# A recurrence, attention and routed experts on one core: warm-up products, chunk 0's sums on VectorE, a re-priced planner, earlier turns of small groups

## The chip, the core and the metric

One core of a Trainium2 chip. The time is that of one execution on the device in microseconds (us); several are made and their median is given. The engines are PE (TensorE), DVE (VectorE), ACT (ScalarE), POOL (GpSimd) and SP (SyncE, which here only issues DMAs). Each runs its own list of instructions in the order in which it was written, and waits for others by semaphores.

## What is computed

The input x has 4 sequences of 1024 tokens with 256 channels. Both halves have the same frame: normalise, compute, normalise, add.

```python
# first half: a recurrence over time, then gates
px = layernorm(x) @ W_state.T + b_state
g  = sigmoid(layernorm(x) @ W_gate.T + b_gate)
state = tanh(px[t] + state)              # 1024 steps, one after the other
x = x + layernorm(g * states)
# second half: causal attention (16 heads of 16 channels), then 4 experts
h = rms(layernorm(x), n1_w); q, k = rms(h @ wq.T), rms(h @ wk.T); v = h @ wv.T
y = layernorm(x) + softmax(causal(q @ k.T / 4)) @ v @ wo.T
w = top2(softmax(rms(y, n2_w) @ gate_w.T))   # two of four experts for each token
y = y + sum(w[e] * expert[e](rms(y, n2_w)))  # the first 64 channels get no addition
x = x + layernorm(y)
```

The experts have two to four layers.

## The kernel before

**Tiling.** Time is cut into 8 chunks of 128 steps. For each chunk: `projections` normalises x (bn_stats L449, scaling L521), turns it (L463, copied to SBUF by ACT and DVE in L472), multiplies it with `wsg` (L534, four banks of 128x512) and evicts states and gates (L552, L548 on DVE). `recurrence` makes the 128 steps: an addition of 128x8 on POOL (L583), then a tanh on ACT (L586; the very first is L579). `gates` makes two wide tanh per chunk (L567). `before` multiplies states by gates (L615), turns them (L623), normalises, adds x, normalises again and turns (L463). `heads` makes q, k and v (L711, L778; turns in L798). Attention runs over 32 tiles (chunk i, sequence b): scores in two layouts (L883), the maximum of one (L968, L975 on DVE), the exponential of the other (L1024 on ACT), sums with v (L1065), and `after` (L1084 to L1128) for the output. `experts_input` routes the chunk's tokens. A tile of chunk i has i + 1 key blocks, so chunk 7 is eight times chunk 0.

**Order.** No loop stands in the program: `Plan.run` writes it out. Every stage is a generator that yields an `Op` (engine, cost in us, priority, events that it reads, buffers that it needs); the planner keeps a clock for each engine and always takes the `Op` that can start first by its clocks, then the one of lower priority. Thus the costs decide only the order in each engine's list; on the chip each engine waits for real events. PE has seven banks of PSUM to hand out (`Banks`). Where the planner sees PE wait for more than 0.8 us between 60 and 420 us on its clock, `fill` puts products into the list that nobody uses (L417).

**Experts.** Tokens are sorted by their pair of experts: six kinds. For each kind, `groups` makes a body for its first 256 tokens, and further groups, each under a branch (L1728), as far as the number of tokens asks for them. A body fetches rows for later groups by indirect DMA from POOL (L1516), turns the next group's rows (`turn`: scaling on DVE L1531, transposes on PE L1538, copy on ACT L1544), and runs the layers (L1561, activations L1622, L1629 to L1638; last layer L1581, added by DVE in L1649). `last` normalises (L1662 to L1678, in between z and r on POOL, L1669 and L1670) and stores the rows by indirect DMA (L1681). A remainder of at most 128 tokens of a kind is its small group, the tail: `rwtail` holds its rows, `xtail` the turned ones. The six tails come after all bodies, each under a branch of its own (L1742):

```python
    for n, c in enumerate(order):
        hint(f"tail{n}", KINDS + c, 0)
        with tc.If(n_of[KINDS + c] > 0, preferred_fallthrough_block=True, label=f"tail{n}"):
            group(c, TAIL, [turn(c, TAIL)])
```

A tail thus fetches nothing (its rows come from the body after its kind's, the last kind's from its own), but it turns its rows itself before its first layer.

Of the kernel before, what the change touches and what calls it, by code (L numbers as in the profile page):

```python
# [18 lines left out]
P = 128  # L19
# [23 lines left out]
def kernel(  # L43
# [43 lines left out]
    nc.vector.tensor_scalar_mul(hb_g, vec[:, 6:8], 0.5)  # L87
# [10 lines left out]
    for arena, group in (  # L98
# [19 lines left out]
        tc, ident, mhalf, hb_g, route, keys, values,  # L118
# [18 lines left out]
LEAST = 0.8  # L137

# [33 lines left out]
class Op:  # L172
    def __init__(self, eng, cost, prio, reads=(), slots=(), banks=0, lag=0.0, either=(), ahead=0.0):
        self.eng, self.cost, self.prio, self.reads = eng, cost, prio, reads
        self.slots, self.banks, self.lag, self.either = slots, banks, lag, either
        self.ahead = ahead


class Plan:
# [13 lines left out]

    def ev(self, *key):
        return self.events.setdefault(key, Ready())

    def start(self, op):
# [7 lines left out]
        for b in self.banks.pick(op.banks):  # L205
            t = max(t, self.banks.free[b])
        return t
# [12 lines left out]
    def run(self, streams):  # L220
# [5 lines left out]
        while waiting:  # L226
# [19 lines left out]
            self.end = t + op.cost + op.lag  # L246
            try:
# [6 lines left out]
def sandwich(  # L254
    ctx, tc, ident, mhalf, hb_g, route, keys, values,
# [76 lines left out]
    def once():  # L332
# [4 lines left out]
        done("loaded")  # L337
        yield Op("DVE", 2.0, 50.0, [ev("st", 0)])
        nc.vector.tensor_copy(ident_h, ident)
# [20 lines left out]
        for p in pads.tiles:  # L360
            yield Op("DVE", 1.2, 50.0)


            nc.vector.memset(p, 0.0)
            nc.vector.memset(p[:, 1, :, HD : HD + 1], 1.0)
# [11 lines left out]
        for e in range(1, E):  # L377
# [3 lines left out]
        nc.gpsimd.memset(mask, 0.0)  # L381
        nc.gpsimd.affine_select(
            out=mask, in_=mask, pattern=[[-1, P]],
            compare_op=ALU.is_ge, fill=NEG, base=0, channel_multiplier=1,
        )
        nc.gpsimd.memset(late[:, : 3 * P], 0.0)

# [16 lines left out]
        )  # L404
        done("once")

    def fill(until):

        now = plan.clock["PE"]
        if not FILLED[0] <= now <= FILLED[1] or until - now < LEAST:  # L410
            return
# [16 lines left out]
    def newton(z, tag):  # L428

        n = z.shape[1]  # L430
# [4 lines left out]
        )  # L435
        nc.vector.tensor_scalar(z, z, -0.5, None, ALU.mult)
        for _ in range(3):
            nc.vector.tensor_tensor(t, y, y, ALU.mult)
            nc.vector.tensor_tensor(t, t, z, ALU.mult)
            nc.vector.scalar_tensor_tensor(y, t, 1.5, y, ALU.add, ALU.mult)  # L440
        return y

    def moments(prio, tiles, tag, reads):

        mv = stat.tile([P, len(tiles), 2], F32, tag=tag, name=tag)
        for n, t in enumerate(tiles):
            yield Op("DVE", 0.6, prio, reads)
            st6 = stat.tile([P, 6], F32, tag="st6", name="st6")
            nc.vector.bn_stats(st6, t)  # L449
            nc.vector.bn_aggr(mv[:, n, :], st6)  # L450
        return mv

    def transposed(prio, srcs, reads, name, ahead=0.0):
# [14 lines left out]
        for cc, (eng, copy) in enumerate(  # L468
            (("ACT", nc.scalar.copy), ("DVE", nc.vector.tensor_copy))
        ):  # L470
            yield Op(eng, 0.65, prio, [ev(name, "in PSUM")])
            copy(to[:, cc, : n * P], banks.tiles[bs[cc]][:, : n * P])  # L472
# [8 lines left out]
    def states(i):  # L481

        both = keys.rearrange("p b (h t) -> p (b h) t", h=NHC)[:, :, i * P : (i + 1) * P]
        return both[:, : NCC * B, :], both[:, NCC * B :, :]

# [10 lines left out]
    def projections():  # L496


        for i in range(NI):
            prio = 4.0 * i - 8.0  # L500
            while i not in xc_of:
                yield Op("DVE", 0.0, prio, [ev("x", i)])
            x_c = xcs.tiles[xc_of[i][1]]
            x_rows = [x_c[:, b, :] for b in range(B)]
            mv = yield from moments(
                prio, x_rows, "mv0", [ev("x", i), *([ev("av", B - 1)] if i >= AT_ONCE else [])]
# [3 lines left out]
            if i:  # L510
                yield Op("DVE", 2.2, prio)
                nc.vector.tensor_scalar(z, mv[:, :, 1], LN_EPS, None, ALU.add)
                r = newton(z, "r0")
# [5 lines left out]
            for b in range(B):  # L519
                yield Op("DVE", 0.35, prio, [ev("r0", i)])  # L520
                nc.vector.tensor_scalar(  # L521
                    x_rows[b], x_rows[b], mv[:, b, 0:1], r[:, b : b + 1],
                    ALU.subtract, ALU.mult,
                )
            done("ln", i)
            to, lnT_ = yield from transposed(prio, x_rows, [ev("ln", i)], f"lnT{i}")
# [3 lines left out]
            for half, dc in ((0, 0), (0, 1), (1, 0), (1, 1)):  # L530
# [15 lines left out]
                yield Op("DVE", 0.68, prio, [ev("pp", i, half, dc)])  # L546
                if half:
                    nc.vector.tensor_scalar(  # L548
                        tile, pb, 0.5, hb_g[:, dc : dc + 1], ALU.mult, ALU.add
                    )  # L550
                else:
                    nc.vector.tensor_scalar(tile, pb, b_s[:, dc : dc + 1], None, ALU.add)  # L552
                give(pp)
                if (half, dc) == (0, 1):
                    done("st", i)
# [14 lines left out]
    def recurrence():  # L570

        prev = None
        for i in range(NI):
            st, _ = states(i)
            last = ev("st", i)
            for t in range(P):
                if prev is None:
                    yield Op("ACT", 0.21, -9.0, [last])
                    nc.scalar.activation(st[:, :, t], st[:, :, t], AF.Tanh)  # L579
                else:  # L580
                    yield Op("POOL", 0.21, -9.0, [last])
                    s = sp.tile([P, NCC * B], F32, tag="s", name="s")
                    nc.gpsimd.tensor_tensor(s, st[:, :, t], prev, ALU.add)  # L583
                    done("s")
                    yield Op("ACT", 0.21, -9.0, [ev("s")])
# [8 lines left out]
            done("rec", i)  # L594

# [4 lines left out]
    def before():  # L600


        for i in range(NI):
# [36 lines left out]
            for b in range(B):  # L640
                row, = yield Op("DVE", 0.8, prio, [ev("r1", i), ev("x1in", i)], [rows])
# [52 lines left out]
    def heads(i, bs):  # L694
# [9 lines left out]
        for k, b in enumerate(bs):  # L704
# [12 lines left out]
            yield Op("ACT", 0.69, prio, [ev("pqk", i, b)])  # L717
# [4 lines left out]
            sq_, = yield Op("ACT", 0.62, prio, (), [sqs])  # L722
# [11 lines left out]
        for k, b in enumerate(bs):  # L734
            if len(bs) > 1:
                yield Op("DVE", 0.8, prio + b)
# [11 lines left out]
                "ACT", 0.69, prio + b,  # L748
                [ev("pk", i, b), *([ev("last read", i)] if i < NI - 1 else [])],
# [11 lines left out]
            yield Op("ACT", 0.69, prio + b, [ev("pq", i, b)])  # L761
# [10 lines left out]
    def value_rows(i, b):  # L772
# [13 lines left out]
        yield Op("DVE", 0.46, prio, [ev("pv", i, b)])  # L786
# [1016 lines left out]
```

## Time and profile before

| | |
|---|---|
| median of 3 runs | 1471.9 us (1470.63 to 1476.9) |
| the profiled execution | 1470.96 us; its span 1469.2 us |
| PE busy | 1311.5 us, 89% |
| DVE, ACT, POOL busy | 896.5, 705.7, 465.5 us |
| mean granted clock of PE | 0.947 |
| last step of chunk 0, 1, 7 | 88.1, 170.5, 741 us |

The span is that of the instructions; the rest of the time lies around it. Products are pipelined and their ends are modelled, so a busy PE is not PE at its peak, and the unused products of L417 count as busy (38.55 us). "<-" in the last brackets of a timeline row names what ended the idle time before it.

### The profile page before, as it was taken

What the parts mean: (1) busy time and instruction counts of PE and PEld (TensorE: products, weight loads), DVE (VectorE), ACT (ScalarE), POOL (GpSimd) and SP (SyncE); (2) the same over time, 40 slices, a digit from 0 to 9 for tenths busy, and PEclk for the clock granted to TensorE, in tenths of its full rate; (3) what the DMA queues carried; (4) which work ended last, traced back from release to release, by engine and by line L of the source; (5) the groups of instructions that cost most, each with busy time, mean ns of one, the idle gap of its engine ahead of it and who ended that gap; (6) DMA issues with size and microseconds to landing.
All of it is one profiled execution on the core that took longest, in us unless ns stands there. A gap on an engine that the chain in (4) does not pass through costs nothing. (4 is left out here: it accounts for less than half of the span.)

```text
span 1469.2 us, 43267 instructions
## 1 busy us (share of the span) xinstructions
PE 1311.5 (89%) x17455; PEld 1020.3 (69%) x17470; DVE 896.5 (61%) x2738; ACT 705.7 (48%) x2144; POOL 465.5 (32%) x1466
## 2 busy tenths in 40 slices
PE   4578797988999998999999999999899999999964
PEld 2235455666676676687677677878688889888764
DVE  5567568599688778778877987784614312113311
ACT  2345545655765765776665455657222222223211
POOL 2433534535444444334311101101233321214321
PEclk8799989999998989998999999999999999999987
DMA  3010010001010000001000100131122120103210
GB/s 128 23 50 2 4 42 17 16 3 46 3 31 17 3 22 28 3 3 46 3 4 5 45 3 4 38 105 62 55 84 64 54 66 26 40 23 83 55 43 5
DMA packets 35917, 49.57 MB, mean 34 GB/s; under 512 B 7638, under 2 KB 27862, under 8 KB 35670
## 3 DMA queue, kind: packets, MB, share of 16 engines
q1 hardware_dynamic: 28774, 25.20, 5.6%
q0 software_dynamic: 6624, 20.62, 5.0%
q8 instruction: 147, 2.41, 0.7%
q14 instruction: 100, 0.82, 0.2%
q10 hardware_dynamic: 272, 0.52, 0.1%
HBM read 32.87 MB, written 13.46 MB: 32 GB/s over the span
## 5 line engine op out<-in xcount | busy, mean ns | idle before, releaser
L1024 ACT ACTIVATE ex<-bank 128x512 f32<-128x512 f32 (+1 forms) x592 | 325.9, 582 | 153.4 <-PE bank L883 87.5
L883 PE MATMUL bank<-keys,q 32*128 32x128 f32 x4608 | 351.9, 293 | 17.4 <-ACT q L762 4.1
L583 POOL TENSOR_TENSOR s<-keys 128x8 f32<-128x8 f32 x1023 | 223.4, 218 | 384.8 <-ACT keys L586 374.1
L883 PE MATMUL bank<-q,keys 32*128 32x128 f32 x4608 | 333.9, 292 | 5.4 <-ACT ex L1024 2.8
L883 PEld LDWEIGHTS bank<-q,keys 32*128 32x128 f32 x4608 | 272.6, 191 | 75.7 <-issue 41.9
L586 ACT ACTIVATE keys<-s 128x8 f32<-128x8 f32 x1023 | 218.5, 214 | 212.1 <-POOL s L583 209.5
L883 PEld LDWEIGHTS bank<-keys,q 32*128 32x128 f32 x4608 | 292.2, 193 | 37.0 <-DVE nm L975 6.3
L975 DVE TENSOR_REDUCE nm<-bank 128x1 f32<-128x512 f32 (+4 forms) x336 | 203.0, 639 | 53.7 <-PE bank L883 44.5
L968 DVE CUSTOM_DVE_ANT_0 bank<-bank,late 128x512 f32<-128x512 f32 (+2 forms) x320 | 188.3, 622 | 48.7 <-PE bank L883 47.4
L1044 POOL TENSOR_SCALAR_AFFINE_SELECT ex<-ex 128x256 f32<-128x256 f32 (+1 forms) x240 | 102.7, 429 | 262.4 <-ACT ex L1024 261.4
L1065 PE MATMUL av<-ex,values 128*17 128x128 f32 x4608 | 175.0, 282 | 3.1 <-issue 1.2
L1561 PE MATMUL bank<-values,keys 128*128 128x256 f32 x568 | 133.5, 381 | 5.9 <-PEq L1728 3.0
L1065 PEld LDWEIGHTS av<-ex,values 128*17 128x17 f32 x4608 | 110.0, 99 | 40.3 <-issue 16.4
L1622 ACT ACTIVATE keys<-bank 128x256 f32<-128x256 f32 (+1 forms) x136 | 50.4, 371 | 149.8 <-PE bank L1561 149.7
L1561 PEld LDWEIGHTS bank<-values,keys 128*128 128x128 f32 x568 | 105.8, 190 | 21.7 <-issue 3.5
L1561 PE MATMUL bank<-keys 128*128 128x256 f32 x384 | 84.8, 379 | 0.0
L1561 PEld LDWEIGHTS bank<-keys 128*128 128x128 f32 x384 | 73.0, 190 | 9.9
L534 PE MATMUL bank<-big,wsg 128*128 128x512 f32 x128 | 64.0, 646 | 5.9 <-ACT big L472 5.9
L711 PE MATMUL bank<-wqk,big 128*128 128x512 f32 x128 | 65.7, 642 | 3.2 <-ACT big L472 3.2
L1649 DVE SCALAR_TENSOR_TENSOR rwnext<-av,rwnext 128x192 f32<-128x192 f32 x24 | 8.9, 414 | 93.4 <-PE av L1581 93.4
L1622 ACT ACTIVATE hid<-bank 128x256 f32<-128x256 f32 x66 | 25.3, 383 | 84.5 <-PE bank L1561 84.5
L1669 POOL TENSOR_SCALAR z<-mv 128x2 f32<-128x2 f32 (+1 forms) x18 | 4.1, 227 | 187.7 <-DVE mv L1663 178.4
(265 smaller groups left out, 1788.2 us busy)
## 6 DMA issues: line engine op xcount, KB each, us to landing
row_d<-xn SPq DMA_DIRECT2D x16, 512.0 KB
xn<-in_x SPq DMA_DIRECT2D x8, 512.0 KB
xc<-in_x SPq DMA_DIRECT2D x7, 512.0 KB
keys<-in_e_l SPq DMA_DIRECT2D x2, 1024.0 KB
keys<-in_e_w SPq DMA_DIRECT2D x2, 512.0 KB
keys<-in_e_down SPq DMA_DIRECT2D x2, 384.0 KB
wsg<-in_w_sg ACTq DMA_DIRECT2D x1, 512.0 KB
xc<-in_x SPq DMA_DIRECT2D x4, 128.0 KB
```

Of the source, the lines that this page charges most:

```text
L534: nc.tensor.matmul(pb, lhsT=wsg[:, cc, half * C + dc * P : half * C + (dc + 1) * P], rhs=lnT[:, cc, :], start=(cc == 0), stop=(cc == NCC - 1),
L583: nc.gpsimd.tensor_tensor(s, st[:, :, t], prev, ALU.add)
L586: nc.scalar.activation(st[:, :, t], s, AF.Tanh)
L711: nc.tensor.matmul(pqk, lhsT=hT[:, cc, b * P : (b + 1) * P], rhs=wqk[:, cc, :], start=(cc == 0), stop=(cc == NCC - 1),)
L883: nc.tensor.matmul(banks.tiles[pbs[j]][:, m * P : (m + 1) * P], lhsT=k if kind == "sT" else q, rhs=q if kind == "sT" else k, start=(m == 0 ...
L968: nc.vector.tensor_tensor_reduce(out=s_, in0=s_, in1=late[:, 4 * P - w :], scale=-1.0, scalar=FMAX, op0=ALU.add, op1=ALU.min, accum_out=by ...
L975: nc.vector.tensor_reduce(by_slot[:, half, h0:h1, 2 * p + j], banks.tiles[pb][:, m0 * P : m1 * P].rearrange("p (h w) -> p h w", h=h1 - h0) ...
L1024: nc.scalar.activation(exs.tiles[ex[1]][:, j, : step.w], banks.tiles[pb][:, : step.w], AF.Exp)
L1044: nc.gpsimd.affine_select(out=d, in_=d, pattern=pattern, compare_op=ALU.is_ge, fill=0.0, base=0, channel_multiplier=-1,)
L1065: nc.tensor.matmul(av[32 * j : 32 * j + HD + 1, hc, :], lhsT=v_all[:, b, kb, 4 * hc + j, :], rhs=exs.tiles[ex[j // 2][1]][:, j % 2, m * P ...
L1561: nc.tensor.matmul(hb[0].tiles[hb[1]][:, :w_], lhsT=w[:, j, m * P : (m + 1) * P], rhs=src[:, j, :w_], start=(j == 0), stop=(j == nk - 1),)
L1622: nc.scalar.activation(to, src, AF.Gelu)
```

## The change

Four parts; the new line of an old one is given where the prediction speaks of it.

1. *Start.* A new stream `begin` casts the identity to bf16 first and lets PE make 100 products of 128x128 with it that nobody uses. `hb_g` (half the gates' bias) is made after chunk 0's statistics instead of at the head of DVE's list. The states of chunk 0 are evicted in two pieces, the first 32 steps first, and the recurrence may begin after the first piece of the second bank. The mask is made first on POOL, and the memsets of the four `pad` tiles go from DVE to POOL. Fillers need the mask.
2. *Chunk 0's steps.* The addition of chunk 0 is made by DVE, of the other chunks by POOL. The projections of chunks 1 to 4, which fall beside it, are cut into small pieces on DVE.
3. *Planner.* Costs are split into the time that an engine is taken and a `lag` until the result is there, and most become smaller. A step announces when the next one is due (`every`: 0.45 us on DVE, 0.52 on POOL); another `Op` of that engine that would run into it waits until after the step, unless it is longer than the whole gap and starts right behind the last step.
4. *Tails.* Their rows are fetched and turned in the bodies of later kinds; the tail's own body turns nothing.

```diff
+SOONEST = 32
+BEFORE_ALL = 100
+BY_VECTOR = 1
+FITS = 0.05
+RIGHT_BEHIND = 0.06
...
+        if op.eng in self.chain and not op.every and op.cost:
+            ended, due, cost = self.chain[op.eng]
+            if t < due < t + op.cost - FITS and not (
+                op.cost > due - ended and t <= ended + RIGHT_BEHIND
+            ):
+                t = due + cost
         return t
...
             self.clock[op.eng] = t + op.cost
             self.end = t + op.cost + op.lag
+            if op.every:
+                self.chain[op.eng] = t + op.cost, t + op.every, op.cost
...
+    def begin():
+        yield Op("DVE", 0.2, -20.0)
+        nc.vector.tensor_copy(ident_h, ident)
+        done("ident")
+        pb, = yield Op("PE", 6.5, -20.0, [ev("ident")], banks=1)
+        for _ in range(BEFORE_ALL):
+            nc.tensor.matmul(
+                banks.tiles[pb][:, :P], lhsT=ident_h, rhs=ident_h, start=True, stop=True
+            )
+        give(pb)
+        yield Op("DVE", 0.2, -7.5, [ev("r0", 0)])
+        nc.vector.tensor_scalar_mul(hb_g, vec[:, 6:8], 0.5)
+        done("hb")
...
-        for p in pads.tiles:
-            yield Op("DVE", 1.2, 50.0)
-            nc.vector.memset(p, 0.0)
...
+        for p in pads.tiles:
+            yield Op("POOL", 1.6, 50.0, [ev("st", 0)])
+            nc.gpsimd.memset(p, 0.0)
...
+            small = 0 < i < AT_ONCE
...
+                pieces = [(slice(0, B), slice(0, P))]
+                if small:
+                    pieces = [(slice(b, b + 1), slice(0, P)) for b in range(B)]
+                elif i == 0 and not half:
+                    pieces = [(slice(0, B), slice(0, SOONEST)), (slice(0, B), slice(SOONEST, P))]
...
-                    yield Op("POOL", 0.21, -9.0, [last])
+                    eng, name, cost = (
+                        (nc.vector, "DVE", 0.17) if i < BY_VECTOR else (nc.gpsimd, "POOL", 0.16)
+                    )
+                    step = 0.45 if name == "DVE" else 0.52
+                    if t == 0:
+                        plan.chain.clear()
+                    yield Op(name, cost, -9.0, [last], every=step, lag=0.0 if name == "DVE" else 0.08)
                     s = sp.tile([P, NCC * B], F32, tag="s", name="s")
-                    nc.gpsimd.tensor_tensor(s, st[:, :, t], prev, ALU.add)
+                    eng.tensor_tensor(s, st[:, :, t], prev, ALU.add)
                     done("s")
-                    yield Op("ACT", 0.21, -9.0, [ev("s")])
+                    yield Op("ACT", 0.11, -9.0, [ev("s")], every=step, lag=0.11)
...
                         yield Op(
-                            "DVE", 0.12 + 1.05e-3 * (m1 - m0) * P, step.at - 1.05,
-                            [ev("s", step.key, p)],
+                            "DVE", 0.1 + 1.0e-3 * (m1 - m0) * P, step.at - 1.05,
+                            [ev("s", step.key, p)], lag=0.08,
                         )
...
                     got = yield Op(
-                        "ACT", 0.2 + 0.83e-3 * step.w, step.at, [ev("sT", step.key, p)],
-                        [] if ex else [exs],
+                        "ACT", 0.05 + 0.84e-3 * step.w, step.at, [ev("sT", step.key, p)],
+                        [] if ex else [exs], lag=0.12,
                     )
...
-            for before in [order[n - 1]] if n else []:
-                then.append(fetch(before, TAIL, 1.0))
-            if n + 1 == KINDS:
-                then.append(fetch(c, TAIL, 1.0))
-            else:
+            if n:
+                got = range(3) if n == 1 else (n + 1,)
+                turned = {2: (0, 1), KINDS - 1: (KINDS - 2, KINDS - 1)}.get(n, (n - 1,) if n > 1 else ())
+                then += [fetch(kind(k), TAIL, 1.0) for k in got]
+                then += [turn(kind(k), TAIL) for k in turned]
+            if n + 1 < KINDS:
                 then.append(turn(kind(n + 1), 0))
...
-            group(c, TAIL, [turn(c, TAIL)])
+            group(c, TAIL, [])
```

The other costs of attention and of the output steps change in the same way (exponential of 128x512: 0.62 in the old list, 0.48 and a lag of 0.12 in the new one; q and k copies 0.69, then 0.58 and 0.1). Costs of PE stay as they were. Nothing that is computed changes.

## The prediction

> **What bounds the kernel now.** The page's slices come first: where is PE (TensorE) short of work, and where is its clock halved?
>
> ```profile
> PE   4578797988999998999999999999899999999964
> PEclk8799989999998989998999999999999999999987
> ```
> A slice is 36.7 us. PE is short in the first eight (to some 290 us) and in the last two. Those two strings tell where to look; the busy times by stretch, cut at the recurrence's own instructions (first tanh 17.43, end of chunk 0 88.1, of chunk 1 170.5, of chunk 7 741), tell how much:
>
> ```profile
> 17.40:88.10 70.70, 41.52 (x105) 19.07 (x104) 42.59 (x161) 29.44 (x132) 28.83 (x142) 0.77 0.11 32
> 170.50:262.00 91.50, 74.12 (x618) 48.38 (x623) 71.59 (x236) 47.72 (x186) 39.22 (x162) 0.91 0.11 30
> 262.00:741.00 479.00, 445.75 (x7554) 330.45 (x7563) 382.53 (x1159) 307.93 (x1050) 206.60 (x789) 0.95 0.06 16
> 741.00:1034.00 293.00, 283.64 (x6603) 225.61 (x6598) 220.32 (x609) 170.74 (x343) 37.16 (x86) 0.99 0.11 33
> 1416.00:1469.20 53.20, 23.12 (x136) 21.48 (x134) 10.91 (x32) 6.28 (x22) 6.75 (x10) 0.70 0.03 10
> ```
> Columns: length, then busy us of PE, its weight loads, DVE (VectorE), ACT (ScalarE), POOL (GpSimd), then the granted clock. Up to about 230 us (the first scores of chunk 1, L883, start at 229.20) the recurrence and the chain behind it set the pace. From there to 1416 PE is the bound: it idles 33.3 of 479 us beside the recurrence, 9.4 of 293 us after it. In the last 53 us it works 23. So time saved before 230 counts almost in full, and at the end in full; between, only PE's idle time and its half clock can be won.
>
> Then the timeline of the start, for the first step's path and for one step:
>
> ```profile
> 9.51 2.30 PE L463 MATMUL bank<-ident,xc 128*128 128x128 f32 x8 [9.51 <-DVE xc L521]
> 11.63 8.41 PE L534 MATMUL bank<-big,wsg 128*128 128x512 f32 x16
> 17.43 0.22 ACT L579 ACTIVATE keys<-keys 128x8 f32<-128x8 f32 x1 [5.85 <-DVE keys L552]
> 18.25 0.20 POOL L583 TENSOR_TENSOR s<-keys 128x8 f32<-128x8 f32 x1 [0.33 <-ACT keys L586]
> 18.48 0.21 ACT L586 ACTIVATE keys<-s 128x8 f32<-128x8 f32 x1 [0.31 <-POOL s L583]
> 18.77 0.20 POOL L583 TENSOR_TENSOR s<-keys 128x8 f32<-128x8 f32 x1 [0.33 <-ACT keys L586]
> ```
> A step of POOL and ACT takes 0.52 us. Last, PE's waits from 1416 on, and the branches of the tails in 1420 to 1430:
>
> ```profile
> PE bank L1538 <- DVE values L1531: 14.6, 2, 10.9
> L1742 PEldq COMPARE_BRANCH  x3: 82/2663/2897, 1418.6 to 1425.0; - x3
> L1742 DVEq COMPARE_BRANCH  x4: 50/56/56, 1424.0 to 1426.7; - x4
> ```
> Two tails run. Before each, PE waits for DVE's scaling of its rows (L1531), 14.6 us in all, though PE stood in the first tail's code at 1425.0.
>
> **A, the first step.** Bank matmuls of 128x512 start 0.85 us apart until 14.3 and 0.43 after: PE is cold for its first 4.8 us. The 100 new products can start when the identity is cast: it is ready at 2.55 (POOL), plus the cast's 0.22 (L339), about 2.95. Their size is not in the trace. The L417 products, four times as wide, come every 0.228 us (13 in 2.97) or 0.43 at half clock, so a quarter is 0.057 or 0.11: 5.7 to 11 us for the 100. Taking 0.107 for 4.8 us (45 products) and 0.057 for the other 55 gives 7.9; they end at 10.9. The normalised rows are ready from 9.1 on, so the products now hold the transposes 1.8 us. Then 8 transposes at 0.13 (1.04 for 8 when warm, at 203.66), ACT's copy 0.59 and DVE's 0.69 behind them, two banks at 1.72, and the eviction of 32 columns instead of 128 (about 0.25 for 0.75): the first tanh at about 15.6, **-1.8**. Products that end by 9.1 give -3.3; at 13.9, +1.2. Moving hb_g behind the statistics takes away DVE's wait for its DMA (5.70), but the last x rows land at 6.49, so that is 0.4, inside this figure. By the Trainium skill ("TensorE: Matmul & The Clock Gate", Part 1), such products stand 107 ns apart for some 38 and 56 ns after; that would be 7.5 us in all, and the sum 0.4 lower.
>
> **B, chunk 0 on DVE.** A step would be ACT 0.22, 0.03 to DVE (1451.08 + 0.28 to 1451.39), an add of 0.16 (as L438) and 0.04 back to ACT (L552 ends 17.39, L579 starts 17.43): 0.45. 127 steps are 57.2 us, now 70.7 (66.0 at 0.52 plus stalls). But DVE's queue is in order, and the changed program's written-out order puts one small piece behind nearly every add. The pieces fit (0.17 + 0.2 < 0.45). What doesn't, less the gap of 0.28: the memsets L340 to L349, 1.78 us, 1.5 over; two gate evictions 0.7; the weight scalings, 0.79 twice, 1.0; the gate product over 96 columns, about 0.6; a memset group, 0.4: 4.2. ACT's two copies and two wide tanh add 0.28 each: 1.1. And the projections of chunks 1 and 2 still meet a cold PE (8 transposes 2.30 at 28.04 and at 46.25); their evictions now stand in the queue ahead of the next add. Price: 1.26 for the transposes and 1.7 for a first bank, each at most; other DVE work covers part; 1.85 taken, 3.7 for two. Sum 66.2, **-4.5** (-8.2 with no cold wait, +2 with the whole price and 0.02 us more a step). The four pad memsets (0.91 each on DVE) go to POOL, which has no steps in chunk 0; used only by chunk 0's heads, after all its steps, they cost nothing. The mask's memsets and select (0.2, 0.29 and 0.41 on POOL) now stand ahead of POOL's z and r of chunk 0; POOL idles from 2.55 to the statistics at about 7.1, so nothing either, and the steps on POOL lose the stall that they made there. A POOL add took 0.45 instead of 0.20 at 32.84 beside DVE's weight scalings. The Trainium skill ("SBUF — State Buffer", "SBUF: two separate sides") makes that an exclusive lock that works the other way too, so POOL's memsets could hold DVE operations; at DVE's 0.91 each that would make the sum 3.6 higher, and no row here shows it.
>
> **C, to the first scores of chunk 1.** ACT operations among chunk 1's steps go from 41 to 40; its 81.6 us are 15 over the pace, so 0.37 each, -0.4. Between chunk 1's gated transposes (L623) and its first scores the old order has 47 unused products, the new one 30. The planner puts them where it sees PE wait; 17 at 0.228 are -3.9. **-4.3** (-8 if the later chain shortens alike, +4 if chunk 0's last output steps, now queued inside this stretch, hold it).
>
> **D, attention.** New costs reorder everything. One count is telling: before the last step stood 298 of 592 exponentials; now 232. PE's work of attention is 352 + 334 + 175 = 861 us, so 96 us of it move from the stretch beside the recurrence (idle 7.0%, clock 0.95) to the one after (3.2%, 0.99): 96 x 0.038 for the idle and as much for the clock, **-7.4**. Ends: the whole 479 us at the later rates, -37; and a loss of 29, priced below.
>
> **E, tails.** Six turns move into bodies that always run: two transposes each, 0.30 (0.60 for four at 1407.23), **+1.8** (5 if the one turning bank makes PE wait); DVE and ACT are idle three quarters there. The six row fetches go to earlier bodies, three of them to the second; POOL issues one in 0.95 (1405.20), is busy 102 of 356 us, and each is turned a body later at the earliest, so that costs nothing unless a fetch for a following kind, queued behind, lands late. In the first tail PE starts at 1425.05 instead of 1428.56, -3.5. The second follows its last product (1438.3) at once instead of at 1443.33, -4.9. Next late is POOL, which reaches the first tail at 1438.0: its r, and DVE's L1675 and L1678, then end at 1439.9, ahead of the second tail's L1632, wanted at 1438.3; 1.2 of that 1.6 taken. **-7.2** (-4 to -8.4).
>
> Sum: -1.8 - 4.5 - 4.3 - 7.4 + 1.8 - 7.2 = **-23.4**. The profiled execution took 1470.96 (span 1469.2 and 1.8 around it; the median of the three is 1471.9): 1447.6.
>
> **Rivals.** *Slower: the recurrence is fed at PE's expense.* The planner now holds an ACT or POOL operation that would run into a due step until after it. An exponential held 0.25 us gives two score banks back late; 232 of them, in pairs that share a wait, are 29 us if PE has no other bank. For it: PE already waits for DVE and ACT in the 479 us. Against: the order's fewer fillers (144 for 154). It decides once PE's idle and half-clock loss in that stretch grow by over 23. Then -16.0 + 29 = +13: 1484. Chance 0.13.
> *No change: DVE's queue gives back chunk 0.* B, C and D are nothing if chunk 0 again takes 70.7 us; A, the turns and the tails leave -7.2: 1463.8. For it: every eviction on DVE waits for a PE at half clock. Chance 0.15.
> *Twice as good: costs that match let PE run through.* 60% of D's far end, -22 instead of -7.4: 1433. Chance 0.12.
> The forecast has 0.60.
>
> About 0.5%, 7.4 us, is what a measurement here can tell from no change. Faster: 0.60 + 0.12 = 0.72; same 0.15; slower 0.13. The range goes down to 1430 (half the third rival lies below) and up to 1480 (most of the first above).
>
> **What would show it.** First tanh near 15.6; chunk 0's steps 0.45 apart and 66 us long; first scores of chunk 1 near 219; last step before 700; PE idle in the stretch up to it below 7%; no wait of PE for L1531's successor after the bodies, and the end 14.5 us after the last product, as now (1454.66 to 1469.2). It is wrong if adds on DVE stand 0.52 apart or wait for PE, if PE's idle beside the recurrence grows, or if a tail still starts after a wait.

## The result: 0.4% slower, where 1.6% faster was forecast

The changed kernel takes 1477.42 us (median; 1473.46 to 1482.49), the kernel before 1472.01 beside it: ratio 1.0036, 95% interval 1.0024 to 1.0047. That is 5.4 us slower instead of 23.4 faster: inside the stated range, on the wrong side of before. The profiled execution took 1477.82 us; its span is 1476.0, 6.8 more than before's.

First the slices of its page, as for before:

```profile
PE   5678788998999999899999999999899999999974
PEclk8788988999999999999999999999999999999997
```

PE is fuller in the first slices (the unused products, partly) and nothing else stands out. The stretches tell more. They are cut at the changed kernel's own marks: first tanh 15.8, last tanh of chunk 0 80.8, of chunk 1 165.3 (their starts; the table below has their ends), of chunk 7 638, then before's 741 (columns as before: length, busy us of PE, its loads, DVE, ACT, POOL, then the clock):

```profile
15.80:80.80 65.00, 34.19 (x94) 14.95 (x92) 51.08 (x292) 29.24 (x131) 0.00 (x0) 0.76 0.08 25
80.80:165.30 84.50, 69.90 (x556) 42.45 (x557) 63.29 (x221) 44.95 (x170) 38.29 (x144) 0.86 0.09 27
165.30:262.00 96.70, 81.33 (x676) 54.07 (x675) 79.37 (x264) 50.06 (x198) 43.87 (x171) 0.88 0.10 29
262.00:638.00 376.00, 349.43 (x5768) 257.41 (x5772) 304.31 (x941) 257.27 (x946) 186.30 (x748) 0.96 0.05 15
638.00:741.00 103.00, 101.27 (x2063) 78.91 (x2055) 76.23 (x209) 60.50 (x117) 18.19 (x40) 0.97 0.06 18
741.00:1036.00 295.00, 282.23 (x6304) 224.41 (x6302) 221.61 (x615) 157.81 (x323) 34.16 (x79) 0.98 0.11 33
```

Chunk 0 takes 65.0 us instead of 70.7, and the last step of all comes at 638 instead of 741. Yet from 262 to the end of attention PE idles 26.6 + 1.7 + 12.8 = 41.1 us, against 33.3 + 9.4 = 42.6 before (there to 1034; the sums are of the unrounded figures). A recurrence that ends 103 us earlier bought PE 1.5 us. The distance to before at marks that both profiles have:

| end of | before | changed | difference |
|---|---|---|---|
| first tanh (start) | 17.4 | 15.8 | -1.6 |
| chunk 0, chunk 1 (steps) | 88.3, 170.7 | 81.0, 165.5 | -7.3, -5.2 |
| attention of chunk 3 | 542.7 | 536.5 | -6.2 |
| attention of chunk 6, 7 | 949.0, 1039.8 | 950.9, 1042.1 | +1.9, +2.3 |
| last product of the bodies | 1416.5 | 1428.7 | +12.2 |
| span | 1469.2 | 1476.0 | +6.8 |

A lead of 5 to 7 us is won by the start, held to 540 us, and gone at 950; the bodies lose another 9.9; the tails give 5.4 back.

The lead in the first 550 us depends on the execution. Five of the kernels below give DVE, ACT and POOL the same order as the changed kernel up to 960 us. In the profiles of four (e_old_tails, e_tails_behind, e_tails_behind_dve, e_route6; e_route6_old runs as the changed one) chunk 1's steps take 80.8 to 82.4 us instead of 84.5, at a granted clock of 0.90 to 0.92 from 81 to 165 us instead of 0.86, and attention of chunk 3 ends at 532.3 to 534.0. So the lead at 540 us is 6 to 10 us; at the end of chunk 6's attention (946.4 to 951.0, for 949.0) it is 2.6 us at most.

### The profile page after: what moved, and what is told of

Its sections match the earlier page's. It is cut to its first block, busy times and chain, and to the rows that moved or that the text cites. A ratio compares the mean times of both kernels' runs of the same rounds, so it can differ in the third digit from the quotient of the medians.

```text
span 1476.0 us, 43633 instructions
## 1 busy us (share of the span) xinstructions
PE 1327.2 (90%) x17568; PEld 1035.8 (70%) x17568; DVE 925.2 (63%) x2955; ACT 705.3 (48%) x2148; POOL 443.7 (30%) x1347
## 5 line engine op out<-in xcount | busy, mean ns | idle before, releaser
L1107 ACT ACTIVATE ex<-bank 128x512 f32<-128x512 f32 (+1 forms) x592 | 321.2, 581 | 144.5 <-PE bank L966 62.7
L966 PE MATMUL bank<-keys,q 32*128 32x128 f32 x4608 | 345.7, 291 | 11.5 <-ACT ex L1107 5.0
L966 PEld LDWEIGHTS bank<-q,keys 32*128 32x128 f32 x4608 | 269.2, 189 | 80.8 <-issue 42.9
L966 PEld LDWEIGHTS bank<-keys,q 32*128 32x128 f32 x4608 | 287.6, 192 | 34.3 <-ACT ex L1107 9.7
L665 POOL TENSOR_TENSOR s<-keys 128x8 f32<-128x8 f32 x896 | 198.2, 221 | 351.0 <-ACT keys L668 284.6
L1644 PE MATMUL bank<-values,keys 128*128 128x256 f32 x568 | 136.7, 387 | 7.7 <-PEq L1813 2.3
```

The costliest lines, as they stand in the source:

```text
L665: eng.tensor_tensor(s, st[:, :, t], prev, ALU.add)
L966: nc.tensor.matmul(banks.tiles[pbs[j]][:, m * P : (m + 1) * P], lhsT=k if kind == "sT" else q, rhs=q if kind == "sT" else k, start=(m == 0 ...
L1107: nc.scalar.activation(exs.tiles[ex[1]][:, j, : step.w], banks.tiles[pb][:, : step.w], AF.Exp)
L1644: nc.tensor.matmul(hb[0].tiles[hb[1]][:, :w_], lhsT=w[:, j, m * P : (m + 1) * P], rhs=src[:, j, :w_], start=(j == 0), stop=(j == nk - 1),)
```

## The experiments

Each kernel is named by its label; ratios are to the kernel before, measured beside it on the same chip. Where e_no_warm, e_before_xn3, e_xn3_route6_old and e_xn3_route6_hold0_old were measured, every kernel, the one before too (1482.1), took some 10 us longer, in the profiled ones behind the end of attention; ratios alone are compared there.

| kernel | median | ratio, 95% interval | chunk 0 / last step end | attention ends |
|---|---|---|---|---|
| changed | 1477.4 | 1.0036 (1.0024 to 1.0047) | 81.0 / 638 | 1042.1 |
| e_old_tails | 1476.9 | 1.0030 (1.0013 to 1.0047) | 81.0 / 635 | 1039.1 |
| e_tails_behind | 1475.7 | 1.0030 (1.0010 to 1.0051) | 81.3 / 637 | 1039.4 |
| e_tails_behind_dve | 1475.9 | 1.0023 (1.0004 to 1.0041) | 81.4 / 635 | 1038.1 |
| e_pool_adds | 1477.7 | 1.0046 (1.0028 to 1.0063) | 90.3 / 644 | 1043.4 |
| e_no_warm | 1489.7 | 1.0051 (1.0032 to 1.0071) | 82.5 / 640 | 1044.0 |
| e_old_costs | 1481.5 | 1.0067 (1.0044 to 1.0090) | 92.1 / 747 | 1046.3 |
| e_no_hold | 1474.9 | 1.0015 (0.9994 to 1.0037) | 89.8 / 685 | 1036.3 |
| e_hold0 | 1480.6 | 1.0038 (1.0022 to 1.0054) | 80.5 / 683 | 1047.0 |
| e_route6 | 1470.5 | 0.9982 (0.9966 to 0.9998) | 81.3 / 637 | 1040.0 |
| e_xn3 | 1473.1 | 0.9997 (0.9982 to 1.0012) | 80.5 / 639 | 1036.4 |

The profile's columns are of one execution each, and executions of one kernel differ by some us; differences under 3 us in the last column say little alone.

**Tails.** e_old_tails takes part 4 back.

```diff
-            if n:
...
-                then += [fetch(kind(k), TAIL, 1.0) for k in got]
-                then += [turn(kind(k), TAIL) for k in turned]
...
+            for before in [order[n - 1]] if n else []:
+                then.append(fetch(before, TAIL, 1.0))
...
-            group(c, TAIL, [])
+            group(c, TAIL, [turn(c, TAIL)])
```

> The changed kernel (1477.4 us) with part 4 undone: small groups' rows are fetched and turned as in the kernel before. Theory 'the tails cost more than they bring': bodies of the experts 345.6 us -> 336 to 338, the section behind the last body's products 47.3 -> 52.7, together some 4.5 less: 1472.9. Rival 'the turns are innocent, the bodies grew for another reason (the clock, the state that attention leaves)': bodies stay at 345, the last section is 5.4 longer: 1482.8.

From the end of attention to the bodies' last product it took 379.3 us for the changed kernel's 386.6, and 50.4 instead of 47.3 behind that: 4.2 less together, as the first theory has it. The medians show only 0.5, within their intervals, and this profile is of the quickest of its twelve executions. So the early tails bring nothing; that they cost something is likely, not shown: with the routing of chunk 6 repaired (below) the old ones are ahead again, 0.9969 for 0.9982, and again within the intervals. In the changed profile PE is busy 371.7 us and idle 14.9 in the bodies, in e_old_tails 367.7 and 11.6. One part of that is seen in the third body of the changed kernel (PE's timeline):

```profile
1191.05 0.38 PE L1621 MATMUL bank<-ident,values 128*128 128x128 f32 x2
1193.04 0.72 PE L1621 MATMUL bank<-ident,values 128*128 128x128 f32 x4 [1.60 <-DVE values L1614]
1194.43 1.11 PE L1621 MATMUL bank<-ident,values 128*128 128x128 f32 x4 [0.68 <-ACT values L1627]
1196.22 4.21 PE L1644 MATMUL bank<-values,keys 128*128 128x256 f32 x9 [0.67 <-ACT values L1627]
```

All turns share one bank. The small groups' turns (two transposes) go first, and the turn that the next body's first product needs (four) is the last work of the body; PE waits three times for the chain scaling, transposes, copy. e_tails_behind puts the small groups' turns behind the others:

```diff
+            got = yield Op("DVE", 0.36, 3.0, [ev("rows", c, g, t), *behind], [] if t else [tbanks["any"]])
...
+                behind = [ev("xT", c, 1)] + ([ev("xT", kind(n + 1), 0)] if n + 1 < KINDS else [])
-                then += [turn(kind(k), TAIL) for k in turned]
+                then += [turn(kind(k), TAIL, behind) for k in turned]
```

> The changed kernel with one edit: in each body the small groups' turns are put behind the turns of the next kind and of the next group (they read those events as well). Theory 'one turning bank: the small groups' turns stand ahead of the turn that the next body's first product needs': bodies 345.6 -> 338, the last section stays near 47: 1469.5. Rival 'the additional work itself (six scalings, twelve transposes, six copies, and the order around them) is the price': bodies stay at 344 to 346: 1477.

The bodies took 382.2, between the two theories: of the 7.3 us that the old tails save there, the order alone gives 4.4 (PE is busy 369.9 us there and idle 12.3). PE's waits for ACT's copy of the next body's rows (1.4 us in the changed kernel) are gone from its list of waits, but its waits for scalings are as long as before, now for the small groups' own rows:

```profile
PE bank L1621 <- DVE values L1614: 2.9, 2, 1.6
```

With the old tails that line is absent. So by these profiles both the additional work in the bodies and its place there have a price; the medians (1.0036, 1.0030 and 1.0030) do not tell the three kernels apart.

The gain that was expected in the tails also came out smaller, for a reason that no step had: POOL's time in branches. Here are PE and POOL in the changed kernel's tails, and POOL's queue at the branches of the tails that are not run (count, shortest, median and longest in ns):

```profile
1436.69 2.90 PE L1644 MATMUL bank<-xtail,keys 128*128 128x128 f32 x12 [7.57 <-DVEq L1827]
1452.28 1.01 PE L1644 MATMUL bank<-keys,values 128*128 128x128 f32 x3 [4.58 <-DVE tnext L1715]
1450.23 0.23 POOL L1752 TENSOR_SCALAR z<-mv 128x1 f32<-128x1 f32 x1 [12.01 <-DMA out<-rwfirst,ids]
L1827 POOLq INC_SWDGE_SEM  x4: 2041/2056/2080, 1443.2 to 1465.1; - x4
```

POOL spends 2.05 us in each skipped branch, reaches the first tail's z at 1450.2 though its input was there at 1446.7, and DVE's `tnext`, which the second tail needs, is queued behind. The forecast had the second tail wait at most 1.6 us, and took 1.2; it was 4.6. e_tails_behind_dve lets DVE compute the tails' r:

```diff
-            yield Op("POOL", 1.1, 3.0, [ev("mv", me)])
+            yield Op(*(("DVE", 2.2) if g == TAIL else ("POOL", 1.1)), 3.0, [ev("mv", me)])
...
+                for _ in range(3):
+                    nc.vector.tensor_tensor(k, r, r, ALU.mult)
+                    nc.vector.tensor_tensor(k, k, z, ALU.mult)
+                    nc.vector.scalar_tensor_tensor(r, k, 1.5, r, ALU.add, ALU.mult)
```

> The changed kernel with the small groups' turns behind the others, as in e_tails_behind (1475.7), and their r (the reciprocal root) made by DVE in 11 small operations instead of two by POOL. Theory 'the second small group waits for POOL, which stands in the branches of the groups that are skipped': its wait of 5.0 us falls to 2.3 (11 x 0.2 stay), the end 2.7 earlier: 1473. Rival 'DVE's order inside the first small group is the wait, not POOL': the wait stays within 1 us, 1475 to 1476.5.

The second tail's wait fell from 5.0 to 1.8, so POOL was the cause; but PE's wait before the first tail grew from 7.7 to 10.1, and the time is the same. In the changed kernel PE comes out of its own branches at 1434.5, DVE out of its last body's branch at 1435.9, and the first tail's product starts at 1436.7. Why this takes longer in e_tails_behind_dve stays open.

**The start.** e_pool_adds moves all sums to POOL (`BY_VECTOR = 0`), e_no_warm leaves one unused product of the 100 (`BEFORE_ALL = 1`).

> The changed kernel with all steps' sums on POOL (BY_VECTOR 0). Theory 'DVE's load gives back what chunk 0 wins': chunk 0 takes 69 to 71 us instead of 65.0, but DVE has 127 sums (20 us) less, chunk 1's steps and the chain behind them are quicker by as much, and the sums with v of the fifth tile start within 1 us of 263.2: 1476 to 1478. Rival, the prediction's step: time before 230 us counts almost in full: the end 5 us later, 1482.

> The changed kernel with one unused product at the start instead of 100. Theory 'a lead at the start is lost where chunks wait for buffers': first tanh 1 to 2 us later than 15.8, the end within 1.5 us of 1477.4. Rival, the prediction's step A: 1.8 us later, 1479.2.

The two answers differ. Without the products the order of everything else on DVE, ACT and POOL is the same, and the profile shows a shift of nearly one size: chunk 0 ends 1.5 us later, chunk 1 1.3, attention 1.9. The ratio is 0.15% higher, which is within the intervals; so the profiles speak for step A's price reaching the end of attention and against the first theory, but the times do not settle it. Without DVE's sums chunk 0 ends 9.3 us later (more than expected: 73.8 us for its steps), and the planner writes another order. DVE has 50.61 of 78.9 us to do in chunk 1's steps instead of 63.29 of 84.5, as the theory has it. But other executions of the changed kernel's order took 80.8 to 82.4 (above), so 2.1 to 3.7 of these 5.6 us are not DVE's load. The first scores of chunk 1 come at 227.6, for 216.4 to 221.8 with DVE's sums, so most of the win is still there; at the end of chunk 6's attention it is gone (949.8 for 946.4 to 950.9), and the times agree within their intervals. So the 5.7 us of step B were lost behind 230 us; that DVE's load gave them back is not shown.

**Planner.** e_old_costs puts all old costs back and drops the hold; e_no_hold drops the hold alone; e_hold0 keeps it for chunk 0.

```diff
+HOLD = False
...
-        if op.eng in self.chain and not op.every and op.cost:
+        if HOLD and op.eng in self.chain and not op.every and op.cost:
```

> The changed kernel with part 3 undone: the planner's old costs, no lag, and nothing held for a due step. Theory 'the recurrence does not pace attention; its last chunks wait for the two buffers of x that chunks two places ahead still hold': the last step goes from 638 back to some 740, the end of attention stays within 4 us of 1036: 1473 to 1481. Rival A, the prediction's step D: attention 7 us longer: 1484. Rival B, 'the new order holds exponentials and loses': 6 or more shorter: below 1471.5.

> The changed kernel with the new costs, but nothing is held for a due step. Theory 'a later recurrence costs only through chunk 0 and 1': chunk 0's steps take 74 to 76 us instead of 65 (as with the old costs, 75.8), the last step is at 660 to 750, and the end is 2 to 4 later: 1479 to 1481. Rival, the prediction's first: holding exponentials costs PE its banks: the end more than 5 us earlier, below 1472.

```diff
+HELD = 1
...
+                    step = step if i < HELD else None
```

> The changed kernel where operations are held for a due step in chunk 0 alone, not in chunks 1 to 7. Without any hold the steps of chunk 0 ended 8.8 us later (89.8 for 81.0), and yet the end was 2.5 earlier (1474.9 for 1477.4), so between lie some 11 to 14 us. Theory 'holding ACT's and POOL's work for steps that nobody waits for costs attention': chunk 0 ends at 81, the last step at 670 to 700, the last x2 of attention 5 to 9 us before the changed kernel's 1042.1: 1468 to 1472. Rival 'each order has its own waits, the hold is not the cause': the end within 2.5 us of 1477.4.

With the old costs the sums on DVE meet other work in its queue, chunk 0 ends 11 us later, and the end is 4 later, between the theory's 1481 and rival A's 1484. Without the hold chunk 0 ends 8.8 later, and the end is 2.5 earlier, with overlapping intervals. With the hold in chunk 0 alone, which should have had the good of both, the ratio is the changed kernel's (1.0038 for 1.0036): that theory fell here. What holding costs can be seen in PE's waits for exponentials from 262 to 1030, first in before, then changed, then e_no_hold (us in total, times, longest):

```profile
PE bank L883 <- ACT ex L1024: 2.4, 5, 0.9
```
```profile
PE bank L966 <- ACT ex L1107: 8.7, 15, 1.3
```
```profile
PE bank L967 <- ACT ex L1108: 1.6, 3, 0.6
```

6.3 us more than before: the first rival's mechanism, at a fifth of its price in this profile. But in each of these orders other waits take part; the last step of the recurrence lies at 638, 683, 685 and 747 us, the end at 1477, 1481, 1475 and 1482, and the one does not follow the other.

**Chunk 6's routing.** The lead is gone by 950 us; behind that, the changed kernel has one long wait that before does not have. PE, changed kernel:

```profile
1011.37 0.92 PE L1203 MATMUL bank<-wo,tee 128*128 128x192 f32 x4
1015.56 0.37 PE L1297 MATMUL bank<-kind,earlier 128*128 128x24 f32 x2 [3.27 <-DVE kind L1284]
1015.77 0.38 PE L1297 MATMUL bank<-kind,every 128*128 128x24 f32 x2
```

The new order puts the routing of chunk 6 at 1008 us (985 before). PE stands for some 25 small DVE operations of it, with a mean granted clock of 0.83 from 1010 to 1020. And POOL asks for the rows of the first experts' body, which that routing names, at 1036.5 (1034.3 before). e_route6 changes one priority:

```diff
-            prio = 4.0 * i + 9.0
+            prio = 4.0 * i + (5.0 if i == NI - 2 else 9.0)
```

> The changed kernel with one priority: the routing of chunk 6 (experts_input) is put four tiles earlier in the planner's order. In the changed kernel PE stands 3.3 us at about 1012 for the counting product of that routing (DVE makes 25 small operations of 0.2 us first), the clock is 0.83 in the 10 us around it, and the last sums with v are 5 us later against before than 30 us earlier. Theory 'that wait is what attention's last stretch loses': no wait over 1 us of that product, clock 1.0 there, attention ends 4 to 5 us earlier: 1473. Rival 'PE and DVE are full, another wait takes its place': the end within 1.5 us: 1476 to 1479.

It is 6.9 us quicker than the changed kernel. The profile shows a second reason that the expectation lacked: rows asked for at 989, and so the first body's products fill the pauses of the last tile, from 1036.6 instead of 1045.9:

```profile
1034.50 0.66 PE L1174 MATMUL bank<-ident,avT 128*128 128x128 f32 x4 [1.64 <-DVE avT L1167]
1034.99 0.60 PE L1621 MATMUL bank<-ident,values 128*128 128x128 f32 x4
1036.10 0.69 PE L1192 MATMUL bank<-ident,row 128*128 128x128 f32 x2 [0.51 <-DVE row L1181]
1036.58 1.92 PE L1644 MATMUL bank<-values,keys 128*128 128x256 f32 x4
```

Before asks for these rows as late as the changed kernel, so this second part of the gain repairs nothing that the change broke; the same edit in before (below) shows it.

**The two buffers.** `before` takes one of two buffers for x (`xns`) for each chunk, and a chunk keeps its buffer until its attention is over and routed. SP's list in the changed kernel, then in before, shows chunk 5's last store and chunk 7's load:

```profile
766.62 0.36 SPq L1232 DMA_DIRECT2D row_d<-xn  x1
...
771.12 0.38 SPq L690 DMA_DIRECT2D xn<-in_x  x1
```
```profile
807.02 0.37 SPq L1149 DMA_DIRECT2D row_d<-xn  x1
811.23 0.38 SPq L607 DMA_DIRECT2D xn<-in_x  x1
```

Chunk 7's steps were over at 638 and at 741. The product of gates and states (L698, L615 before) does not read what is loaded, but it stands behind that load in the same stream, so the planner places it later too. On DVE, changed kernel and before:

```profile
773.21 1.27 DVE L698 SCALAR_TENSOR_TENSOR keys<-keys 128x768 f32<-128x768 f32 x2
```
```profile
809.10 1.33 DVE L615 SCALAR_TENSOR_TENSOR keys<-keys 128x768 f32<-128x768 f32 x2
```

The same holds for chunk 6 (steps over at 563 and 643; product at 676 and 667, behind chunk 4's end at 673 and 661). So from chunk 5 on the recurrence was not what the chain waited for, in either kernel. In the changed kernel, chunk 4's last tile is even 13 us later than before, and with it chunk 6's chain 9: the scores of chunk 6 begin no earlier than before, and the lead is gone. PE's products show the same: at 741 us the changed kernel is ahead by 277 recorded products of those from 262 on (7831 for 7554), at 800 us it is 200 behind (8847 for 9047). e_xn3 has a third buffer, and one fewer for exponentials to make room:

```diff
     xns = slots(2, [P, B, C], "xn")
+    xns = Slots(xns.tiles + [ip.tile([P, B, C], F32, name="xn2")])
-    exs = slots(6, [P, 2, 4 * P], "ex", ip)
+    exs = slots(5, [P, 2, 4 * P], "ex", ip)
```

> The changed kernel with three buffers for x of a chunk instead of two, and five for exponentials instead of six (for the room). Theory 'from chunk 5 on a chunk's chain waits for the buffer that the chunk two places ahead holds until its attention is over, so a quicker recurrence brings nothing': chunk 7's product of gates and states starts before 700 instead of at 773, DVE is no longer 95% busy from 760 to 800, and attention ends 5 to 8 us earlier: 1470 to 1472. Rival 'the chain is only moved, PE's and DVE's work stays': the chain is early as well, but the end is within 2 us: 1475.5 to 1479.5; slower than that if the sixth buffer for exponentials was needed.

Attention ends 5.7 earlier, the time is 4.3 shorter: a little less than the theory said, and chunk 7's product came at 745, not before 700. The buffer still held it: chunk 4's attention ended at 694.4, but its rows were turned for the routing at 743.2 only, and chunk 7's load follows at 744.4. And in that profile PE waits 3.5 us for the routing again. The two repairs have to be tried together, and on the kernel before as well, to see what the change itself is worth.

**Both repairs, on both kernels.** The edits are those shown above, put together: "old" is the old tails, "hold0" the hold in chunk 0 alone. First the routing, in the kernel before and in the changed one with old tails:

```diff
-            prio = 4.0 * i + 9.0
+            prio = 4.0 * i + (5.0 if i == NI - 2 else 9.0)
```

> The kernel before with chunk 6's routing four tiles earlier and nothing else. Theory 'the first experts' rows are asked for at 1034 because that routing is late, and the pauses of the last tile can be filled by their products': rows asked for before 1000, first product of the bodies at 1036 instead of 1043.6, end 4 to 7 earlier: 1465 to 1468. Rival 'what was lost is the 3.3 us wait that the changed kernel alone has': 1471 to 1473.

> The changed kernel with chunk 6's routing four tiles earlier (1470.5 alone) and the tails of the kernel before. Theory 'both losses add': the early tails cost 0.5 (by the medians) to 4.2 us (by the profile's sections): 1466.5 to 1470. Rival 'the routing's gain contains that loss': 1470.5 to 1472.

> The three edits together: routing of chunk 6 earlier, tails as before, hold in chunk 0 alone. If the theory of the hold is right, 1461 to 1466: 4 to 8 below the same kernel with the hold in all chunks. If each order has its own waits, anything from 1466 to 1474.

Then the third buffer (with five buffers for exponentials, as above), in before alone, and with the routing in the others:

```diff
+    xns = Slots(xns.tiles + [ip.tile([P, B, C], F32, name="xn2")])
```

> The kernel before with three buffers for x of a chunk (and five for exponentials). Theory 'the two buffers pace the later chunks in both kernels': chunk 6's product of gates and states, at 667 behind a step that ended at 643, comes 15 to 25 earlier, chunk 7's, at 809 behind a last step at 741, comes 50 or more earlier; the end 2 to 4 earlier: 1468.5 to 1470.5. Rival 'only the changed kernel's order needs it': within 1.5 of 1472.5, or later for want of the sixth buffer for exponentials.

> The changed kernel with three buffers for x, chunk 6's routing earlier, tails as before. Theory 'the buffers lose what the start wins': 3 to 4 below e_route6_old (1467.8), as e_xn3 was below the changed kernel: 1464. Rival 'both edits repair the same loss': 1467 to 1469.

> The same with the hold in chunk 0 alone. Theory 'the buffers lose what the start wins': 3 to 4 below e_route6_hold0_old (1465.5): 1462. Rival 'each order has its own waits': 1463 to 1470.

> The kernel before with the third buffer for x and chunk 6's routing earlier, and nothing of the change but that. Theory 'with the buffers out of the way the earlier chunk 0 and the quicker recurrence count': within 0.4% of before (the third buffer alone gave 1.0011, the routing alone 0.9979), 0.997 to 1.000. Rival 'the two repairs are the whole gain': 0.983 to 0.989, like the kernel that has the change's parts 1 to 3 as well.

> The same kernel as e_xn3_route6_hold0_old. Its ratio to the kernel before was 0.9833. If that holds: 0.980 to 0.987, some 1447 to 1455 where the kernel before takes 1472.5; if it was that call alone: 0.990 to 0.996, as the same kernel with two buffers (0.9955).

Ratios to the kernel before (interval half-widths 0.001 to 0.0023); the last two columns are the change's parts 1 to 3 with the old tails:

| repairs | before | parts 1 to 3 | parts 1 to 3, hold in chunk 0 only |
|---|---|---|---|
| none | 1 | 1.0030 | not run |
| routing of chunk 6 | 0.9979 | 0.9969 | 0.9955 |
| third buffer | 1.0011 | not run | not run |
| both | 0.9965 | 0.9893 | 0.9833; again 0.9817 |

The routing alone gave before 3.5 us, under the 4 to 7 expected; the third buffer alone gave it nothing, where 2 to 4 were expected, and the rival held: chunk 7's product comes 54 us earlier, at 755, eight behind the last step at 747, and the end does not move (1.0011). So an earlier start of that chain is no gain by itself in before. With both repairs before gains 0.35%, so the rival that the two repairs are the whole gain fell. The change's parts 1 to 3 are worth +0.3% (slower) with none of them, -0.1% with the routing, -0.7% with both, and -1.5% with both and the hold in chunk 0 alone: 0.9817 against 0.9965, measured beside each other. The -0.1% lies within the intervals. The two repairs together gave parts 1 to 3 more than the sum of what each gave (0.9893 for some 0.993). Limiting the hold, worth nothing without repairs, is then worth 0.6%; that the other waits had hidden it fits, but was not shown. The last kernel takes 1445.7 us (1441.99 to 1449.87), less than before and the changed kernel. In it and in before with the same repairs, PE in the stretches up to the end of attention:

```profile
262.00:638.00 376.00, 355.16 (x5872) 262.81 (x5876) 303.08 (x944) 249.40 (x873) 177.95 (x681) 0.95 0.06 18
638.00:741.00 103.00, 101.17 (x2143) 77.95 (x2139) 80.06 (x191) 68.16 (x184) 29.96 (x103) 0.99 0.05 13
```
```profile
262.00:638.00 376.00, 352.87 (x5655) 257.88 (x5656) 298.01 (x926) 236.88 (x814) 165.99 (x625) 0.94 0.06 17
638.00:741.00 103.00, 99.34 (x1890) 75.66 (x1892) 86.32 (x236) 68.77 (x231) 40.59 (x159) 0.98 0.05 13
```

5872 + 2143 recorded products against 5655 + 1890 up to 741 us: more work done at the same mark, and attention ends at 1022.1 instead of 1041.3. Chunk 7's load is now at 721.8, still 36 us behind the last step, so a wait is left there. How much of the 1.5% belongs to each of the three parts was not separated, and the fifth exponential buffer was not tried without the third for x. Every edit also rewrites the planner's order, and orders without a repair differ by up to 0.5% here (1.0015 to 1.0067); the 1.5% is beyond that, but it is one order's.

## Why the prediction was wrong

**A, the first step: right.** The products take 7.32 us (7.9 reckoned) and end at 10.2; the first tanh comes at 15.83 for 15.6. The Trainium skill's figures ("TensorE: Matmul & The Clock Gate", Part 1) gave 7.5, nearer than the estimate from quarter-sized products. Over all profiles with these products the first tanh comes at 15.4 to 16.9, in e_no_warm at 17.29, in the kernels with before's order at 17.2 to 18.1.

**B, chunk 0: right in size, wrong in worth.** 65.0 us for 66.2. POOL's memsets, which might have held DVE, end at 15.40, ahead of the steps; POOL is busy for 0.00 us in them. The memsets that were said to stand 1.5 us too long before the second step do so (they fill DVE from 16.51 to 18.28):

```profile
16.44 0.22 ACT L668 ACTIVATE keys<-s 128x8 f32<-128x8 f32 x1 [0.39 <-DVE s L665]
16.51 0.48 DVE L369 MEMSET av<- 128x512 f32 x1
18.32 0.17 DVE L665 TENSOR_TENSOR s<-keys 128x8 f32<-128x8 f32 x1
18.52 0.22 ACT L668 ACTIVATE keys<-s 128x8 f32<-128x8 f32 x1 [1.87 <-DVE s L665]
```

**C: the step "time saved before 230 counts almost in full" failed.** The first scores of chunk 1 came at 221.84 for 219, and at 216.4 to 218.0 in the four other profiles of the same order: the lead of A, B and C, 10.6 us by the forecast, was there with 7.4 to 12.8 (before: 229.20). It did not count: at the end of chunk 6's attention 2.6 us at most were left of it. DVE's load, priced in chunk 0 alone, is 199.7 us up to 262 instead of 171.8 (127 sums and the split pieces), but no wait was found that this load costs. By the profiles the lead was lost behind 540 us (D).

**D: the failed step that weighed most.** It took a count, exponentials before the last step (it was 232, as said), for work that PE could do at better rates. The count fell because the last step came 103 us earlier, but nothing waited for that step. Before's profile had it: chunk 4's steps end at 434.9 and their second product starts at 435.1, but chunk 5's wait from 533.6 to 549.7, chunk 6's from 643.4 to 667.1, chunk 7's from 741.0 to 809.1. That growing distance should have been read before anything was priced on the last step. The change's order also moved chunk 6's routing to where PE waits for it; the forecast looked for stalls at the steps, not at the rare stages. With both waits repaired and the hold in chunk 0 alone, attention ends 19.2 us earlier than in before with the same repairs; with the hold in all chunks, as forecast, only 7.4 (1033.9 for 1041.3). That the 19.2 are near the 18.0 of A to D together is luck as far as is known: the kernel is another one, and D's own working (idle and clock of moved work) was not tested.

**E: both terms mis-sized.** Bodies +9.9 for 1.8 (the bound given for a wait on the one turning bank was 5; undoing part 4 gives 7.3 of the 9.9 back); tails -5.4 for -7.2, since the second tail waited 4.6 us for what stood behind POOL's branches, not 1.2. Both tails still started after a wait, which the forecast had named as a sign of being wrong.

Of the rivals, the first (holding) is there at 6.3 us instead of 29, below the 23 from which it decides; with both repairs, holding in chunks 1 to 7 costs 0.6%, some 9 us. The second fell: chunk 0 stayed quick on DVE. The 0.13 for "slower" rested on the first alone; no rival had a wait on a buffer.

## What to carry to other kernels

Before pricing a quicker producer, list for each of its results when it is ready and when its consumer starts: where that distance grows, something else (here a buffer held by older work, seen in SP's list) is what the consumer waits for, and a quicker producer brings nothing there. Closing the distance alone need not be a gain either (e_before_xn3). A change of a planner's costs is a new order, whose rare stages (here one routing, placed 24 us later) can cost more than the common ones gain; look at them one by one. A gain that vanishes may only be covered: test it again with the covering wait removed, on both kernels. And compare profiles of several executions before a difference of a few us is put down to an order.

## What the hardware showed beyond expectation

- The spread of one kernel goes with the granted clock: of 113 executions of the kernel before (those at 1482.1 left out), the 40 at a mean clock of 0.946 or more took 1470.6 us on average, the 13 below 0.942 took 1475.6. The Trainium skill ("TensorE: Matmul & The Clock Gate", Part 1) says that the window that gates the clock runs freely, so that the number of slow products differs between runs of one kernel; these figures agree with that, but they show only that clock and time go together here, not that this is the reason.
- POOL spends 2.05 us in each branch that skips a small group's block (INC_SWDGE_SEM, four times 2.04 to 2.08 us): twice what it takes to issue one indirect DMA (0.99 us at 1437.24).
- In e_before_xn3, measured where all kernels took some 10 us longer, PE stood once for 4.5 us in the bodies without a releaser that the profile shows; the cause is open.

```profile
PE bank L1562 <- issue: 4.5, 1, 4.5
```
